# Moving the last result of a Strassen projection into tiles that an operand sum has left, with its residual loaded through another queue

## The chip, the cores and the metric

The kernel runs on one core of a Trainium2 chip, in one launch. The metric is the device time of that core in microseconds (us); runs of the same kernel are compared by their median. The profile is one such execution, recorded instruction by instruction.

## The reference

For each of 16 images, `x` is (512 channels, 1024 pixels) in f32. Group normalisation over 8 groups, a 1x1 convolution to queries, keys and values, attention with 4 heads of 128 channels over the 1024 pixels, a 1x1 output projection, and the residual:

```python
xn = ((xg - mu) * rsqrt(var + EPS)) * gamma + beta
q, k, v = split(einsum('oc,bchw->bohw', qkv_w, xn) + qkv_b, 3)
attn = softmax(einsum('bhnd,bhmd->bhnm', q, k) * scale)
out = einsum('bhnm,bhmd->bhnd', attn, v)
out = einsum('oc,bchw->bohw', proj_w, out) + proj_b
return x + out
```

## The kernel before

**The loop.** The work is written as 512 steps: 16 images, 4 heads, 8 blocks of keys. Each step has two halves, and each half issues one score matmul (`s`, L789, 128x512), its exponential on ScalarE (ACT, `p`, L795), and for the step before one weighted-sum matmul (`po`, L885). Every f32 matmul appears as two passes in the profile. Between these, `plan_head` hands out "units" of other work: queries and keys (`qk_`), values (`v_`), the projection of the image before (`pp_`), and the statistics and normalisation of the image after. A scheduler then orders the instructions of each engine by priorities (`tc.high_priority`) and by its own estimates, so the order on an engine is not the order of the source.

**Two Strassen levels.** `two_levels` multiplies a 512x512 weight by 512x1024 data with two levels of a Strassen scheme: seven outer products, done in four groups `OUTER = ((1, 5), (2, 6), (7, 4), (3,))`, numbered 0 to 3, and in each group seven inner products. `strassen` runs these in the order p1, p2, p6, p5, p7, p4, p3. Two PSUM banks, x and y, take the products; ACT copies x aside (`kept_copy`, L458, the tiles `pp_u` and `pp_p`), and VectorE (DVE) adds the parts into SBUF tiles `R` (`out_`, L584, `pp_r`). The inner operand sums t1 to t4 are DVE subtractions in `make_sum` (L534, `pp_t`, `qk_t`). Weight groups come by DMA on the queue of SyncE (SP), L371: two tiles a group, `w0` and `w1`, each in a pool of two buffers, so a load waits for the weights of two groups before.

**The outer sums of o.** The projection's data are the four heads' outputs (`os_`), and the outer sums t2, t3, t4 of them lie in single-buffered tiles of `tpool`: `ot20, ot21, ot30, ot31, ot40, ot41` (`halves`). The outer t4, which is `ot40` and `ot41`, is the operand of the outer product 4 alone, so only group 2 reads it: `ot40` holds the inner blocks b11 and b12, `ot41` holds b21 and b22. No other part of the kernel uses the tags `ot40` and `ot41`, and they are written again in the next image.

**The projection's results.** `proj_groups` gives eight 128x512 results an image: c11 (two), c22 and c21 (four), c12 (two). For each, `prepare` loads the residual block of `x` from DRAM into a tile (L756), `finish` adds R and the bias into it (L769), adds the second R (L772), and stores it (L773). `ready` calls `prepare` in the unit of p5 of group 1 (c11), group 2 (c22, c21) and group 3 (c12). All eight tiles come from `ypool`, tag `y`, four buffers used in turn, which the values' tiles `vt` and `vu` share. The load of a tile therefore waits until the store of the tile four places earlier has landed: c21 waits for c11, and c12 waits for c22. The loads and stores are issued on the queue of GpSimd (POOL), in order with POOL's small power instruction `rstd` (L67) of the next image's normalisation and with the loads of x and the copies of qk_t and v to DRAM.

**What stands around it.** `prepare` runs in the second head's part of an image (`plan_head`, h = 1) for images 0 to 14; the projection of image 15 is another function, `last_projection`. In the same stretch DVE takes part in the normalisation (L50 to L78), the running sums of p (`tot`, L803), and the first inner sums of the next image's queries and keys, `qk_t` (L534), without which TensorE (PE) can't start the products p5 of that group, `qk_y<-qk_t` (L564). ACT normalises the next image there (L85).

Of the kernel before, what the change touches and what calls it, by code (L numbers as in the profile page):

```python
# [10 lines left out]
F32 = mybir.dt.float32  # L11
# [5 lines left out]
P = 128  # L17
# [4 lines left out]
HALF = 512  # L22
# [140 lines left out]
def fast_path(ctx, tc, x, sources, out, consts, flag, dims):  # L163
# [6 lines left out]
    nc = tc.nc  # L170
# [10 lines left out]
    tpool = ctx.enter_context(tc.tile_pool(name="t", bufs=1))  # L181
# [7 lines left out]
    ypool = ctx.enter_context(tc.tile_pool(name="y", bufs=4))  # L189
# [556 lines left out]
    def proj_groups(b):  # L746

        ys = {}

        def place(which, r):  # L750
            return 2 * (int(which[1]) - 1) + r, int(which[2]) - 1

        def prepare(which, r):
            o, half = place(which, r)
            t = ys[which, r] = ypool.tile([P, HALF], F32, tag="y", name=f"y_{b}_{o}_{half}")
            dma = nc.gpsimd.dma_start(t, x[b, ts(o, P), ts(half, HALF)])  # L756

            tc.add_manual_dep(
                dma.ins, last_eviction[b].ins.name,
                mybir.DependencyInfo(  # L760
                    mybir.DependencyClass.Sync, mybir.DependencyReason.DATA
                ),
                reason="residual",
            )

        def finish(which, r, a, c):
            o, half = place(which, r)
            t = ys.pop((which, r))
            nc.vector.scalar_tensor_tensor(  # L769
                t, a, projb_sb[:, o : o + 1], t, ALU.add, ALU.add  # L770
            )
            nc.vector.tensor_add(t, t, c)  # L772
            nc.gpsimd.dma_start(out[b, ts(o, P), ts(half, HALF)], t)  # L773

        return two_levels(f"pp_{b}", "proj", b, lambda: ob[b], finish, prepare=prepare)
# [6 lines left out]
    def where(s):  # L782
        bh, j = divmod(s, NB)
        return (*divmod(bh, HEADS), j)
# [327 lines left out]
    for s in range(steps + 1):  # L1112
        units = []
        if s < steps:
            b, h, j = where(s)
# [159 lines left out]
```

## Time and profile before

| | |
|---|---|
| median of 7 runs | 3189.69 us (3188.1 to 3192.7) |
| the profiled execution's own time | 3190.44 us |
| its span, first to last instruction | 3188.7 us |
| PE busy | 3157.4 us, 99% of the span |
| DVE busy | 2632.9 us, 83% |
| ACT busy | 1443.7 us, 45% |
| POOL busy | 527.6 us, 17% |
| granted TensorE clock | 1.000 |
| `y<-in_x` loads on POOL (L756) | 120, of 256 KB, 3.9 us from issue to landing (median) |
| `w_proj<-kept_proj` loads on SP (L371) | 120 |

Time lies outside the span too: 3190.44 - 3188.7 = 1.7 us. In the lines of the profile, a row has the start in us, the length in us, the engine, the source line, the operation, and `out<-in` by the names of the tiles with their numbers left out; `x2` means that two equal instructions are merged. In brackets stands how long the engine was idle before it and what ended the idle time. One image takes some 196.3 us.

### The profile page before, as it was taken

The page shows a single profiled execution, that of the slowest core. Times are in us where ns is not written, and L with a number is a line of the kernel's source. Part 1 is how long each engine was busy: PE and PEld are TensorE (multiplying, and loading weights), DVE is VectorE, ACT ScalarE, POOL GpSimd, SP SyncE. Part 2 cuts the span into 40 slices and gives each one's busy share as a digit, 9 for nine tenths or more (in the row PEclk, how much of TensorE's full clock was granted, in tenths as well). Part 3 has the DMA queues.
Part 4 walks back from the last instruction along what each step waited for, and adds up shares of the span by engine and source line. Part 5 has one row for each costly group of instructions (what it writes and reads, how often), then busy time and mean ns, then how long its engine had stood idle before and what let it go on. Part 6 is the DMA issues. An engine that isn't in the chain of part 4 may idle for free.

```text
span 3188.7 us, 34047 instructions
## 1 busy us (share of the span) xinstructions
PE 3157.4 (99%) x10474; PEld 2183.5 (68%) x10474; DVE 2632.9 (83%) x4625; ACT 1443.7 (45%) x2709; POOL 527.6 (17%) x922
## 2 busy tenths in 40 slices
PE   8999999999999999999999999999999999999999
PEld 6566676776766766667666676667666676766764
DVE  8878978788887888878888787987879878788784
ACT  2535435354353543534435454453534545344342
POOL 0011221111211112211122111222112221122200
PEclk9999999999999999999999999999999999999999
DMA  5655554546545455454554546555455554555531
GB/s 168 208 185 160 185 177 144 179 143 199 166 156 168 155 186 175 157 166 145 193 171 162 172 135 196 166 173 173 134 182 169 175 180 131 183 158 186 180 126 41
DMA packets 209387, 526.92 MB, mean 165 GB/s; under 512 B 32816, under 2 KB 65840, under 8 KB 209200
## 3 DMA queue, kind: packets, MB, share of 16 engines
q1 hardware_dynamic: 128992, 276.88, 28.3%
q0 software_dynamic: 66240, 212.39, 19.8%
q10 hardware_dynamic: 13968, 35.41, 3.5%
q8 instruction: 86, 1.41, 0.2%
q14 instruction: 101, 0.83, 0.1%
HBM read 389.56 MB, written 135.00 MB: 165 GB/s over the span
## 4 chain that ended last, share of the span: by engine, by line
PE 87%; DVE 5%; issue 3%; DMA 2%; ACT 2%; POOL 1%; SPq 0%; POOLq 0%; DVEq 0%
PE po L885 24%; PE s L789 24%; PE qk_x L564 12%; PE qk_y L564 9%; PE v_x L564 6%; PE v_y L564 4%; PE pp_x L564 4%; PE pp_y L564 3%; ACT x L85 1%; DVE pp_r L631 1%; DMA y<-in_x 1%; POOL rstd L67 1%; DVE pp_r L584 1%; DVE tot L803 1%; DMA out_y<-y 1%
## 5 line engine op out<-in xcount | busy, mean ns | idle before, releaser
L885 PE MATMUL po<-p,v 128*128 128x512 f32 x2048 | 1048.9, 594 | 0.0
L789 PE MATMUL s<-qk,qk 128*128 128x512 f32 x2048 | 1047.1, 593 | 1.3 <-ACT p L795 1.3
L795 ACT ACTIVATE p<-s 128x512 f32<-128x512 f32 x1024 | 610.8, 597 | 945.5 <-PE s L789 903.8
L885 PEld LDWEIGHTS po<-p,v 128*128 128x128 f32 x2048 | 602.9, 303 | 316.8 <-issue 212.1
L803 DVE TENSOR_TENSOR tot<-tot,p 128x1024 f32<-128x1024 f32 x385 | 469.2, 1219 | 161.6 <-ACT p L795 161.6
L789 PEld LDWEIGHTS s<-qk,qk 128*128 128x128 f32 x2048 | 387.6, 190 | 89.2 <-issue 28.0
L564 PEld LDWEIGHTS qk_x<-qk_t,w 128*128 128x128 f32 x1344 | 250.6, 190 | 171.3 <-issue 76.6
L564 PE MATMUL qk_x<-qk_t,w 128*128 128x256 f32 x1344 | 357.3, 382 | 1.1 <-ACT qk_u L458 1.1
L458 ACT COPY qk_u<-qk_x 128x512 f32<-128x512 f32 (+1 forms) x256 | 136.3, 533 | 231.9 <-PE qk_x L564 227.4
L728 POOL DMA_DIRECT2D vd<-vu x120 | 66.6, 556 | 906.8 <-DVE vu L720 903.1
L584 DVE TENSOR_TENSOR qk_r<-qk_y,qk_u 128x512 f32<-128x512 f32 (+1 forms) x256 | 158.4, 619 | 36.1 <-ACT qk_u L458 21.8
L564 PE MATMUL pp_x<-pp_t,w_proj 128*128 128x256 f32 x630 | 169.3, 385 | 6.0 <-ACT pp_u L458 5.8
L773 POOL DMA_DIRECT2D out_y<-y x120 | 66.2, 551 | 615.8 <-DVE y L772 585.8
L733 POOL DMA_DIRECT2D v<-vd x240 | 140.5, 592 | 163.8 <-DMA vd<-vu 61.3
L584 DVE TENSOR_TENSOR v_r<-v_y,v_u 128x512 f32<-128x512 f32 (+1 forms) x120 | 75.7, 631 | 110.6 <-ACT v_u L458 80.3
L564 PE MATMUL v_x<-v_t,w_v 128*128 128x256 f32 x630 | 166.6, 381 | 0.0
L538 POOL DMA_DIRECT2D kept_t<-qk_t x240 | 129.2, 540 | 224.4 <-DVE qk_t L534 158.4
L564 PEld LDWEIGHTS pp_x<-pp_t,w_proj 128*128 128x128 f32 x630 | 115.4, 190 | 73.2 <-issue 22.2
L564 PEld LDWEIGHTS v_x<-v_t,w_v 128*128 128x128 f32 x630 | 118.4, 190 | 55.3 <-issue 19.1
L564 PE MATMUL qk_y<-x,w 128*128 128x256 f32 x512 | 141.8, 379 | 0.0
L663 DVE SCALAR_TENSOR_TENSOR qk<-qk_r,qkb_sb,qk_r 128x512 f32<-128x512 f32 x192 | 137.7, 745 | 1.6
L458 ACT COPY v_u<-v_x 128x512 f32<-128x512 f32 (+1 forms) x124 | 66.3, 535 | 160.4 <-PE v_x L564 130.3
(204 smaller groups left out, 4485.0 us busy)
## 6 DMA issues: line engine op xcount, KB each, us to landing
kept_t<-qk_t POOLq DMA_DIRECT2D x180, 256.0 KB, 3.0
w<-kept SPq DMA_DIRECT2D x90, 512.0 KB, 4.0
v_t<-kept_t SPq DMA_DIRECT2D x180, 256.0 KB, 2.8
w<-kept SPq DMA_DIRECT2D x90, 384.0 KB, 3.6
rinv<-row ACTq DMA_DIRECT2D x63, 512.0 KB, 4.8
x<-in_x POOLq DMA_DIRECT2D x60, 512.0 KB, 4.8
vd<-vu POOLq DMA_DIRECT2D x120, 256.0 KB, 3.1
v<-vd POOLq DMA_DIRECT2D x240, 128.0 KB, 4.1
```

What stands on the lines that cost most here:

```text
L458: nc.scalar.copy(t[n][:, :width], t["x"][:, :width])
L538: nc.gpsimd.dma_start(t, to)
L564: nc.tensor.matmul(acc[:, ts(i, Q)], have["w"][t][:, i, slot, :], inner(i, bn), start=(first and i == 0), stop=True, skip_group_check=True,)
L584: nc.vector.tensor_add(dst, view(a), view(c))
L663: nc.vector.scalar_tensor_tensor(st[b, h][:, ts(half, HALF)], a, qkb_sb[:, i : i + 1], c, ALU.add, ALU.add)
L728: nc.gpsimd.dma_start(rows[which][ts(h, P), :], u)
L733: nc.gpsimd.dma_start(vs[b, pair][ts(q, BLK), half].rearrange("m h (k i) j -> m (h k) (i j)", k=n), rows[which].rearrange("(k m) (q e) -> ...
L773: nc.gpsimd.dma_start(out[b, ts(o, P), ts(half, HALF)], t)
L789: nc.tensor.matmul(sc, ks[b, h][:, ts(j, P)], qs[b, h][:, ts(half, HALF)], start=True, stop=True)
L795: exps[s] = nc.scalar.activation(ps[s][:, ts(half, HALF)], sc, AF.Exp, scale=SCALE)
L803: added[b, h, j] = nc.vector.tensor_add(tot[b, h][:, i], tot[b, h][:, i], ps[s][:, i])
L885: nc.tensor.matmul(po[b, h][:, i], v_block(b, h, j), ps[s][:, i], start=(j == 0), stop=(j == NB - 1),)
```

## The change

The two c12 results of images 0 to 14 no longer take tiles of `ypool`. They take tiles of `tpool` under the tags `ot40` and `ot41`, and their residuals are loaded by a DMA on SP's queue. The loads of the other six results, the additions and all stores are as they were (stores on POOL's queue). `ypool` now gives 22 tiles an image in place of 24. Lines behind the edit move down by six: the load is L762, the additions are L775 and L778, the store is L779.

```diff
         def prepare(which, r):
             o, half = place(which, r)
-            t = ys[which, r] = ypool.tile([P, HALF], F32, tag="y", name=f"y_{b}_{o}_{half}")
-            dma = nc.gpsimd.dma_start(t, x[b, ts(o, P), ts(half, HALF)])
+
+            own = which == "c12"
+            t = ys[which, r] = (tpool if own else ypool).tile(
+                [P, HALF], F32, tag=f"ot4{r}" if own else "y", name=f"y_{b}_{o}_{half}"
+            )
+
+            eng = nc.sync if own else nc.gpsimd
+            dma = eng.dma_start(t, x[b, ts(o, P), ts(half, HALF)])
 
             tc.add_manual_dep(
                 dma.ins, last_eviction[b].ins.name,
```

## The prediction

> **What bounds the kernel now.** The first view is the page's busy times, the second its chain of work that ended last.
>
> ```profile
> PE 3157.4 (99%) x10474; PEld 2183.5 (68%) x10474; DVE 2632.9 (83%) x4625; ACT 1443.7 (45%) x2709; POOL 527.6 (17%) x922
> PE 87%; DVE 5%; issue 3%; DMA 2%; ACT 2%; POOL 1%; SPq 0%; POOLq 0%; DVEq 0%
> ```
>
> PE sets the time, so a change pays only where PE stands still. The third view is the waits, for PE alone:
>
> ```profile
> PE pp_x L564 <- ACT pp_u L458: 5.8, 14, 0.4
> PE qk_y L564 <- DVE qk_t L534: 3.6, 3, 1.8
> ```
>
> Outside the start these two are nearly all: 14 waits of 0.41 us, one in each image but the last, and three for DVE's qk_t. To see where DVE was late I read the groups of instructions for the tile y:
>
> ```profile
> L769 DVE SCALAR_TENSOR_TENSOR y<-pp_r,projb_sb,y 128x512 f32<-128x512 f32 x120 | 87.9, 748 | 6.3 <-DMA y<-in_x 5.5
> ```
>
> DVE waited 5.5 us for residual loads in all. The timeline says which ones. Image 5, by engine:
>
> ```profile
> 1321.74 1.15 POOL L773 DMA_DIRECT2D out_y<-y  x2 [5.69 <-DVE y L772]
> 1325.06 0.54 POOL L756 DMA_DIRECT2D y<-in_x  x1 [0.58 <-DMA out_y<-y]
> 1326.42 0.54 POOL L756 DMA_DIRECT2D y<-in_x  x1 [0.82 <-DMA out_y<-y]
> 1331.65 0.75 DVE L769 SCALAR_TENSOR_TENSOR y<-pp_r,projb_sb,y 128x512 f32<-128x512 f32 x1 [1.95 <-DMA y<-in_x]
> 1334.00 0.70 PE L564 MATMUL qk_y<-qk_t,w 128*128 128x256 f32 x2 [1.81 <-DVE qk_t L534]
> ```
>
> and image 6:
>
> ```profile
> 1523.25 1.20 POOL L756 DMA_DIRECT2D y<-in_x  x2 [0.47 <-DMA out_y<-y]
> 1527.27 1.47 DVE L769 SCALAR_TENSOR_TENSOR y<-pp_r,projb_sb,y 128x512 f32<-128x512 f32 x2
> 1529.86 0.42 DVE L534 TENSOR_TENSOR qk_t<-x 128x256 f32<-128x256 f32 x1
> 1529.90 1.13 PE L564 MATMUL qk_y<-qk_t,w 128*128 128x256 f32 x4
> ```
>
> Both loads are c12's: they wait until c22's stores have landed, and reach POOL only 4.0 us before DVE wants them (1523.25 to 1527.27). The same loads take 3.9 us to land at the median. So it is a race: in image 6 it is just won, in image 5 lost by 1.95 us, and 1.81 of it reaches PE. Image 6 shows one thing more. Four passes of this kind take 1.03 us elsewhere and 1.13 here: the second pair of `qk_y` waits some 0.1 us for `qk_t`, which ends at 1529.86 + 0.42 = 1530.28. DVE is just in time even where no load is late. The length of an image, from one `rstd` to the next, is in the chain in order of time:
>
> ```profile
> 1314.16 1.88 POOL rstd L67
> 1512.48 1.89 POOL rstd L67
> 1708.83 1.89 POOL rstd L67
> ```
>
> Image 5 takes 198.32 us, image 6 196.35. The later `rstd` give 196.30, 196.45, 196.31, 197.97, 196.81, 196.27. I take 196.30 as an image with no late load.
>
> **The late loads.** DVE's waits at L769 are 0.24, 0.29, 0.28, 1.95, 1.42, 0.45 us in images 1, 3, 4, 5, 10, 11, and 0.90 in image 14. Images 3, 4, 5, 10 and 11 lie 0.44, 0.36, 2.02, 1.67 and 0.51 us above 196.30. Images 1 and 2 are together 0.83 above, of which I give the wait in image 1 some 0.3; the rest is none of this. The wait in image 14 has no `qk_t` behind it and PE shows no wait: zero, at most 0.9. Sum 0.3 + 0.44 + 0.36 + 2.02 + 1.67 + 0.51 = **5.3 us**.
>
> **Whether they go.** In the built program's order on SP, the first c12 load stands between the two weight loads of projection group 3, the second between those of the next image's query group 0. Before, these lie at 1494.93 and 1504.42, and at 1507.86 and 1514.34 in image 6. The first load must wait for the last readers of `ot40`: group 2's p1 (PE, 1497.32 to 1498.35) and its t3 sums (DVE, to 1498.28), so it goes at about 1498.4, while the load behind it can't go before 1504.42 anyway. The second waits for group 2's p3, which is what `w1` behind it waits for too (1514.34): that load goes one issue, 0.32 us, later. Its weights are first read at the `qk_x` of 1533.46, 19 us on, so this costs nothing; if that cover were gone it would cost 0.32 an image, 4.5 in all.
>
> What the loads must beat: DVE's addition for the first is moved forward in the built order, into the slot of an outer sum of o (L280) at 1510.97, 12.6 us after the issue; the second's stands behind the first's second addition, about 1528.2, 13.9 us after. SP's loads of 256 KB have medians of 2.8 (`v_t<-kept_t`) and 3.2 us (`w_proj`), all loads of L371 2.2 to 9.1, the residuals on POOL 2.7 to 10.4. The highest is inside 12.6, so I take a wait of zero and a gain of 5.3.
>
> The Trainium skill, "DMA: Bandwidth & Descriptors", section "Issuing engines are not separate DMA queues", speaks against such a change: DMAs from any engine run on the same 16 DMA engines, and spreading them saves only issue time. By that rule alone this change is worth nothing, and the execution would stay at 3190.4. The rows say that the wait is for a tile to come free, not for a queue; by them it is 5.3.
>
> **Issue work.** POOL loses 30 issues of 0.54 us, SP gains 30 of 0.32. Neither is on the chain, and c21's last store, `kept_t` and `vd` on POOL stand behind two instructions fewer, which wait for DVE (903.1 us at L728). Zero.
>
> **DVE's new order.** The addition takes the place of the sum of o, that sum the place of a t3 sum of group 3, t3 that of t4, t4 that of the first `qk_t`; the first `qk_t` goes behind the second c12 addition. Counted from one row's start to the next, an addition takes 0.66, a sum of o 0.61, an inner sum 0.34. By the second `qk_t` the same instructions have run, so it ends at 1530.28 as before. In between, `sh` (L78, 1515.86) comes 0.05 + 0.27 = about 0.3 later. Behind it ACT is busy without a break to 1524.5, so the copy `pp_p` ends at about 1518.15 in place of 1517.83, and PE's p6, at 1518.02, may wait 0.3.
>
> **PE's new order.** In group 3, p4 and p3 go behind one `po` and one `s` more. The 0.41 wait (0.67 with what follows it: from `s` at 1521.47 to `po` at 1523.43 is 1.96, where 0.86 + 0.43 is the rule) goes, since `po` fills it until `pp_u` is there. So PE saves 0.67 and loses 0.3, and comes to the second `qk_y` pair about 0.4 early, and there it waits for 1530.28. What is late next is `qk_t`, and the gain is given back. Bounds an image: a loss of 0.3 if p6's wait is not swallowed, a gain of 0.67; times 14, +4.2 and -9.4. I take zero, since the row of 1529.90 shows the wait for `qk_t` already.
>
> **Sum.** 3190.44 - 5.3 = 3185.1. The profiled execution is 0.75 above the median of 3189.69, but a median run loses its own late loads too and should fall to the same floor, so the prediction is **3185.1 us**, 0.14% below the median. What this measurement can tell from no change is 0.2%, 6.4 us: faster begins below 3183.3, slower above 3196.1.
>
> **Rivals.** (1) *The floor holds*, as above: 3182 to 3187.5. Below 3185.1 lie 0.7 of excess that I gave to nothing (0.53 in images 1 and 2, 0.05 + 0.15 in two others), 0.9 of image 14 and 0.1 an image if the wait in the row of 1529.90 shrinks, 3.0 in all; above it lies about half of p6's price. (2) *PE keeps what p4 saves*: DVE is not what ends the stretch, because with no late loads it runs ahead by itself. For it: DVE has a 0.93 us gap before L69 where it could gain. Against it: that gap ends with POOL's `rstd`, which stands behind DVE's own chain, and the 1.13 row. 0.41 to 0.67 in 14 images is 5.7 to 9.4: 3175.7 to 3179.4. (3) *The load is hidden but another takes its place*: c21's loads (POOL, 1505.24 and 1509.70) still wait for stores, and the next operand after c12 is late by as much, or p6 waits the full 4.2: 3189 to 3190.4. For it: PE is 99% busy and DVE has no slack. Against it: c21's are first used at 1520.27 and 1521.87, 12 us or more after their issue. (4) *Slower*: the first load lands after DVE's early slot. DVE then stands at 1510.97 with the chain `pp_r`, `ve`, `rstd`, `sh` behind it, and ACT's normalisation behind that; each us is one of PE, 14 times. It decides from a landing of 12.6 us; slower by 0.2% needs 11 us over the floor, 0.8 an image, a landing of 13.4. At 14 us it would be 3185.1 + 14 x 1.4 = 3205. Against it: nothing in the rows above 10.4. That the edit does nothing is excluded: the load stands on SP in the built order.
>
> **Chances.** (1) 0.60, of which 0.15 lies below 3183.3; (2) 0.20; (3) 0.11; (4) 0.09. Faster is 0.15 + 0.20 = 0.35, same 0.45 + 0.11 = 0.56, slower 0.09. The range from 3178.5 to 3188.5 holds (1) whole, about a half of (2) and little of (3), and leaves out (4).
>
> **What would show it.** Right: no wait of L775 for `y<-in_x`; c12's loads issued on SP about 14 us before the `rstd` of the image (1498.4 against 1512.48) and 2 us after it; PE's three waits for `qk_t` of 1.8, 1.4 and 0.3 gone, but many of 0.2 to 0.5 at the same place, and none of `pp_x` for `pp_u`; images of 196.3 throughout. Wrong: images of 195.8 with no wait at `qk_y` (2), waits for other tiles (3), or DVE idle ahead of `ve` for `y<-in_x` (4).

## The result, and the profile after

The changed kernel takes 3181.79 us (median of 13 runs, 3180.58 to 3183.52), the kernel before 3191.18 us in the same comparison (median of 33, 3186.52 to 3197.61). The ratio is 0.9971, 95% interval 0.9964 to 0.9979: faster by 0.29%. The prediction was 3185.1 us in a range of 3178.5 to 3188.5; "same" was held likelier than "faster", and by the bound of 0.2% set there it is faster. The profiled execution took 3181.52 us with a span of 3179.7 us (before: 3190.44 and 3188.7).

Busy times and the chain of work that ended last, from the page of the kernel after:

```profile
PE 3157.4 (99%) x10474; PEld 2182.9 (69%) x10474; DVE 2630.0 (83%) x4625; ACT 1441.8 (45%) x2709; POOL 512.4 (16%) x892
PE 87%; DVE 10%; issue 1%; POOL 1%; DMA 1%; ACT 0%; SPq 0%; POOLq 0%; DVEq 0%
```

PE does the same 3157.4 us of work in a span that is 9.0 us shorter: only standing time went. PE's waits for `qk_t` (engine, tile and line, released by what; us in all, times, longest; the view lists waits of 0.15 us and more):

```profile
PE qk_y L564 <- DVE qk_t L534: 2.2, 14, 0.2
```

The line of 14 waits for `pp_u` is gone. In place of three long waits for `qk_t` there are fourteen of 0.15 us. The group of DVE's additions into y has no releaser left and 0.6 us idle, where it showed 6.3 us idle, 5.5 of it for `y<-in_x`:

```profile
L775 DVE SCALAR_TENSOR_TENSOR y<-pp_r,projb_sb,y 128x512 f32<-128x512 f32 x120 | 88.5, 748 | 0.6
```

`rstd` in the chain in order of time, from image 5 on:

```profile
1310.61 1.89 POOL rstd L67
1506.88 1.89 POOL rstd L67
1703.10 1.89 POOL rstd L67
```

196.27 and 196.22 us, where 198.32 and 196.35 stood. The timeline of image 6, SP and then DVE and PE (start, length, engine, line, operation, tiles, count):

```profile
1492.75 0.33 SPq L762 DMA_DIRECT2D y<-in_x  x1
1498.75 0.32 SPq L371 DMA_DIRECT2D w_proj<-kept_proj  x1
1502.20 0.32 SPq L371 DMA_DIRECT2D w<-kept  x1
1508.68 0.33 SPq L762 DMA_DIRECT2D y<-in_x  x1
1505.31 0.75 DVE L775 SCALAR_TENSOR_TENSOR y<-pp_r,projb_sb,y 128x512 f32<-128x512 f32 x1
1522.48 0.75 DVE L775 SCALAR_TENSOR_TENSOR y<-pp_r,projb_sb,y 128x512 f32<-128x512 f32 x1
1524.08 0.42 DVE L534 TENSOR_TENSOR qk_t<-x 128x256 f32<-128x256 f32 x1
1512.49 0.70 PE L564 MATMUL pp_x<-pp_t,w_proj 128*128 128x256 f32 x2
1524.55 0.70 PE L564 MATMUL qk_y<-qk_t,w 128*128 128x256 f32 x2 [0.15 <-DVE qk_t L534]
```

The two c12 loads go 14.1 us before `rstd` (1506.88) and 1.8 us after it, and are wanted 12.6 us (1505.31) and 13.8 us (1522.48) after their issue. Before, the issue was 4.0 us ahead of the use. The second `qk_y` pair starts at 1524.55, just after `qk_t` ends at 1524.50. The row of 1512.49 is p6, the product that now waits a little for `pp_p`.

**Where the 9.0 us of span came from.** The span is cut at the `rstd` of image 0 and at the last one, 13 images later. Up to the first cut the two profiles differ by 1.6 us (331.03 before, 329.42 after), in the 13 images by 6.7 (2557.92 and 2551.25), behind the last cut by 0.7 (299.73 and 299.00). Part of that is chance, as the further profiles show.

### The profile page after: what moved, and what is told of

Same layout as the page of the kernel before. It is cut to its first block, busy times and chain, and to the rows that moved or that the text cites. A ratio compares the mean times of both kernels' runs of the same rounds, so it can differ in the third digit from the quotient of the medians.

```text
span 3179.7 us, 34036 instructions
## 1 busy us (share of the span) xinstructions
PE 3157.4 (99%) x10474; PEld 2182.9 (69%) x10474; DVE 2630.0 (83%) x4625; ACT 1441.8 (45%) x2709; POOL 512.4 (16%) x892
## 4 chain that ended last, share of the span: by engine, by line
PE 87%; DVE 10%; issue 1%; POOL 1%; DMA 1%; ACT 0%; SPq 0%; POOLq 0%; DVEq 0%
PE po L891 24%; PE s L795 24%; PE qk_x L564 12%; PE qk_y L564 9%; PE v_x L564 6%; PE v_y L564 4%; PE pp_x L564 4%; PE pp_y L564 3%; DVE y L778 2%; DVE tot L809 2%; DVE y L775 2%; DVE pp_r L584 1%; DVE pp_r L631 1%; POOL rstd L67 1%; DVE o L901 1%
## 5 line engine op out<-in xcount | busy, mean ns | idle before, releaser
L779 POOL DMA_DIRECT2D out_y<-y x120 | 66.0, 550 | 632.0 <-DVE y L778 629.8
```

## The experiments

All are medians against the kernel before in the same group of runs; it had medians of 3190.3 to 3191.2 in the four groups. The kernel after was run in the first group alone, so a difference of one or two us between it and a variant is better read from the images than from the medians. "Image" is the mean of the 13 images in the profile; "loads" is DVE's wait at c12's first additions.

| kernel | median, us | ratio (95%) | image, us | loads, us |
|---|---|---|---|---|
| before, three profiles | 3190.3 to 3191.2 | | 196.76, 196.91, 196.69 | 5.5, 7.0, 4.2 |
| after | 3181.79 | 0.9971 (0.9964 to 0.9979) | 196.25 | 0 |
| tiles alone | 3182.0 | 0.9976 (0.9966 to 0.9985) | 196.24 | 0 |
| queue alone | 3187.77 | 0.9991 (0.9982 to 1.0000) | 196.75 | 4.5 |
| both, but the old wait | 3188.23 | 0.9994 (0.9985 to 1.0003) | 196.60 | 4.9 |
| both, order of before | 3182.32 | 0.9975 (0.9966 to 0.9985) | 196.31 | 0 |
| no c12 load at all | 3183.62 | 0.9979 (0.9970 to 0.9988) | 196.29 | - |
| load still later | 3211.14 | 1.0064 (1.0049 to 1.0080) | 198.10 | 51.3 |
| one more addition on DVE | 3184.40 | 0.9983 (0.9974 to 0.9992) | 196.47 | 0 |
| first sums urgent | 3184.27 | 0.9983 (0.9974 to 0.9993) | 196.43 | 0 |
| first sums 4 places earlier | 3183.50 | 0.9978 (0.9969 to 0.9987) | 196.39 | 0 |
| first sums 12 places earlier | 3183.97 | 0.9982 (0.9973 to 0.9991) | 196.40 | 0 |

### Tiles alone, queue alone

The change has two halves. The first kernel keeps the tiles `ot40` and `ot41` and loads through POOL's queue as before:

```diff
-            eng = nc.sync if own else nc.gpsimd
+            eng = nc.gpsimd
```

> c12 in the tiles ot40 and ot41, its residuals loaded on POOL's queue as before the change; PE, DVE and ACT have the changed kernel's order. (A) The gain comes from loads that no longer wait for c22's stores: they go 12 us ahead of their use, so 3.3 to 5.2 us of landing on POOL do no harm, and the time is the changed kernel's, 3181.8 within 1 us. (B) The gain comes from SP's queue, on which these loads land in 2.5 to 2.9 us: without it the kernel goes back towards 3191. (C) The gain comes from the order of DVE and PE, which is here as changed: 3181.8 too. The second load stands behind rstd on POOL, 13 us before its use, and costs nothing by any of them.

The second keeps SP's queue and takes the tiles from `ypool` again:

```diff
-            t = ys[which, r] = (tpool if own else ypool).tile(
-                [P, HALF], F32, tag=f"ot4{r}" if own else "y", name=...
+            t = ys[which, r] = ypool.tile([P, HALF], F32, tag="y", name=...
```

> c12 in ypool's tiles as before, its residuals loaded on SP's queue; the order on DVE, PE and ACT is that of the kernel before. The loads still wait for c22's stores and can go only 4.0 us ahead of their use. (A) The wait for the tile is there, so the late loads are too: 3188 to 3191. (B) On SP they land in 2.5 to 2.9 us, inside the 4.0: no DVE wait for y<-in_x, and 3182 to 3183. (C) The order is the old one, with the 0.41 us wait of PE for pp_u in each image: 3191, or 3187 where only the late loads go. By my forecast, which gave the queue nothing: 3190.

Tiles alone give 3182.0 us, within 0.2 us of the whole change. Queue alone gives 3187.77 us, some 2.9 below before, with an interval that ends at 1.0000. DVE's waits in the kernel with the queue alone:

```profile
DVE y L775 <- DMA y<-in_x: 4.5, 4, 2.5
```

So the loads stay late when only their queue changes. The tile that comes free early is the cause. The Trainium skill, "DMA: Bandwidth & Descriptors", section "Issuing engines are not separate DMA queues", by which alone the prediction had the whole change at nothing, agrees with this half: less than 0.2% for the queue.

One of the four late loads cost more than its wait. In image 2 PE stood for 2.33 us, and behind that the granted clock was 0.50 from 743 to 745 us and 0.76 from 745 to 747; the image is 4.24 us over 196.30, some 1.9 beyond the wait. In the next kernel PE stood for 2.67 us in the same image, the clock stayed at 1.00, and the image is 2.92 us over.

### Both, but the old wait

The kernel after, with each c12 load made to wait for the c22 store that it waited for before:

```diff
+            if own:
+                tc.add_manual_dep(
+                    dma.ins, stores["c22", r].ins.name, ...
```

> The changed kernel, but each c12 load is made to wait until the store of the c22 result of the same half has landed, as it had to before; the order on DVE, PE and ACT falls back to that of the kernel before. (A) The wait is back, and so is the time: 3188 to 3191. (B) SP's landing of 2.5 to 2.9 us is inside the 4.0 us: 3182 to 3183, as with the queue alone. (C) 3187 to 3191.

3188.23 us, and 4.9 us of waiting for the loads. With the new tiles and the new queue but the old moment of issue most of the gain is lost: some 2.5 of 8.7 us stays, as with the queue alone, and the interval holds 1. Four loads are late, in images 2, 6, 10 and 14 as with the queue alone. It is the moment that counts.

### Both, in the order of before

The new order on DVE could be a gain of its own. This kernel is the one after, with c12's first additions queued behind the last sum that stood ahead of them, which puts DVE's instructions into the order of before:

```diff
+            with ExitStack() as late_:
+                if which == "c12":
+                    late_.enter_context(tc.issue_after(added[b + 1, 1, NB - 1].ins))
...
```

> The changed kernel's tiles, queue and early loads, but c12's first additions are held behind the last running sum of p, so that DVE, PE and ACT have the order of the kernel before. (A) and (B): no late load, so 3181.8 plus at most 0.05 us in each of 14 images: 3181.5 to 3183. PE waits 0.41 us for pp_u in each image again and 0.1 for qk_t, in place of 0.15 for qk_t. (C) 3187 to 3191.

3182.32 us; images of 196.30, against 196.25. PE's waits:

```profile
PE pp_x L564 <- ACT pp_u L458: 5.8, 14, 0.4
```

The 14 waits for `pp_u` are back, the 14 for `qk_t` are gone, and the image is 0.05 us longer. What p4 saves in the new order is lost again at p6 and at `qk_y`, but for 0.05 us. It also confirms 196.30 as the length of an image with no late load in the old order.

### No load, and a later load

The kernel before without c12's residual load, and the kernel after with loads that wait for the last c21 store:

```diff
+            if which == "c12":
+                return
...
-                t, a, projb_sb[:, o : o + 1], t, ALU.add, ALU.add
+                t, a, projb_sb[:, o : o + 1], c if which == "c12" else t, ALU.add, ALU.add
```

> The kernel before, but the c12 results load no residual: the tile still comes from the four of ypool and still waits until c22's store of it has landed, and the first addition takes the second R in place of the residual (c12's residual is left out of the output; as many DVE instructions of the same shapes, in the order of before). It leaves the wait for the stores and takes the load's own 3 to 5 us away. Theory A (only the landing of the load against DVE's addition matters, a store that has landed 4 us earlier costs nothing): no wait of DVE for y, none of PE for qk_t beyond 0.2, the 14 waits of 0.4 for pp_u stay; the middle 13 images 2552.0 as in the kernel after with its old order, median about 3182.3. Rival (the stores on POOL's queue, or the tiles of ypool, hold something else up as well): images stay above 196.3 and the median at 3184 to 3190.

Images of 196.29 with the wait for c22's stores still there: a store that has landed in time costs nothing, and the excess over 196.30 goes with the loads (a small part of it was not c12's, as the further profiles of before show). The median of 3183.62 is 1.3 us over the one expected, with intervals that overlap.

```diff
+            if own:
+                tc.add_manual_dep(
+                    dma.ins, stores["c21", 1].ins.name, ...
```

> The kernel after, but the two c12 loads wait until the last c21 store of the image has landed (in the frame of image 6 about 1528, where DVE wants the first at 1527.3 in the order of before). Landing takes another 3.3 to 4.5 us, so the first addition is 4 to 5 us late in each of 14 or 15 images. Theory A (PE follows DVE one for one there, as in the images 5 and 10 of the kernel before, where 1.95 and 1.42 us of waiting cost 2.02 and 1.67): 14 x 4.1 to 14 x 5, so 57 to 70 us above 3181.8, 3239 to 3252. Rival (the order is planned anew around the late load and DVE has other work to put first, or PE's queue holds other units): a part of it is hidden, 3190 to 3225.

3211.14 us: the rival's 3190 to 3225 held, not the 3239 to 3252 of one for one. DVE waited 51.3 us for the loads, and the median rose by 29.3. From its waits, and from DVE's timeline in image 6:

```profile
PE qk_y L564 <- DVE qk_r L584: 11.9, 15, 0.9
1536.41 0.42 DVE L534 TENSOR_TENSOR qk_t<-x 128x256 f32<-128x256 f32 x1
1538.09 1.28 DVE L280 TENSOR_TENSOR xt<-x,x 128x512 f32<-128x512 f32 x2
1542.49 0.75 DVE L783 SCALAR_TENSOR_TENSOR y<-pp_r,projb_sb,y 128x512 f32<-128x512 f32 x1 [3.12 <-DMA y<-in_x]
```

The scheduler knew of this wait, and put most of the inner sums and two sums of x (L280) ahead of the late addition. PE then waits for the next thing behind it, `qk_r`, by 0.8 us an image, and 13 times for `qk_t` at `qk_x`, 2.9 us in all. So a late load cost about its full length where it came by chance into an order that does not allow for it (1.95 us of waiting and 2.02 of image in image 5 of the kernel before), and somewhat over half where the order was made for it.

### What is left at qk_t

After the change PE waits 14 times for `qk_t`. One more DVE addition of 128x512 ahead of it, in each image (c21's first half gets its second R twice):

```diff
+            if which == "c21" and r == 0:
+                nc.vector.tensor_add(t, t, c)
```

> The kernel after with one more DVE addition of 128x512 (some 0.6 us) at the first c21 result of each image, ahead of the first qk_t of the next image (c21's first half gets its second R twice). If DVE ends the stretch, as the prediction says (qk_y waits 0.2 for qk_t in 14 images), PE waits 0.6 more in each: 14 x 0.6 = 8.4, about 3190. If DVE has slack there that the 0.2 hides, or the new order puts other work behind: 3182 to 3185.

3184.40 us, 2.6 more and not 8.4; the image is 0.2 us longer where DVE has 0.6 us more to do. The second `qk_t` ends 0.6 us later against the `rstd`, as expected, but PE's order changed with it. From PE's timeline:

```profile
1525.40 0.67 PE L564 MATMUL qk_y<-qk_t,w 128*128 128x256 f32 x2 [0.15 <-DVE qk_t L534]
1525.90 1.02 PE L797 MATMUL s<-qk,qk 128*128 128x512 f32 x2
1526.76 0.59 PE L564 MATMUL qk_y<-qk_t,w 128*128 128x256 f32 x2
```

A score matmul of 0.86 us now stands between the two pairs of `qk_y`, and the wait is at the first pair. How late DVE is there depends on the planned order, not on its amount of work alone.

Then the other way round, the sums earlier. In three steps: urgent (shown), 4 places, 12 places:

```diff
-            for i in range(n):
...
+            with ExitStack() as early:
+                if sums == "keep" and g == 0 and m == "t1":
+                    early.enter_context(tc.high_priority(URGENT))
+                for i in range(n):
+                    nc.vector.tensor_sub(to[:, i, :], inner_block(g, i, a), inner_block(g, i, c))
```

> The kernel after, with the first inner sums of each image's queries (group 0, t1) planned ahead of the other DVE work as urgent, so that qk_t does not stand behind c12's additions. If the 14 waits of 0.2 at qk_y are all that DVE costs PE in the stretch, they go and nothing else comes: 14 x 0.2 = 2.8 less, 3179. If the order after the sums makes other work late by as much (sh, and ACT's normalisation behind it; or ot for the next group): 3181 to 3186. The order on PE is planned anew as well, so a new wait elsewhere may decide: then above 3186.

> The kernel after with the first inner sums t1 of an image's queries planned 4 places earlier: DVE's order stays as it is, on PE one score matmul goes ahead of the qk_y pair, and the second qk_y behind the next qk_x, so that the wait of 0.2 us for qk_t is filled. If PE's place before qk_t is all that is left, 14 x 0.15 to 0.2, so 2 to 3 us: images of 196.05 to 196.15, 3179 to 3180. If the next operand is as late (the qk_x that now comes earlier), the images stay at 196.25 and the median at 3181.8.

> The kernel after with the same sums planned 12 places earlier: on DVE both stand ahead of the last three c12 additions, and PE takes the four products p5 and p7 in turn ahead of the score matmul. If DVE's end at qk_t was the last wait of the stretch, it goes: 14 x 0.2 = 2.8 us, 3179. If PE needs the operand of p7, which is now early as well, before DVE has it, a wait of 0.2 to 0.4 comes back at qk_x, as it did with the urgent sums: 3182 to 3184.

(With 4 and 12 places the number stands for URGENT, and with 4 only the second of the two sums was given the priority.) PE's waits for the stretch, in the kernels urgent, 4 places and 12 places:

```profile
PE qk_x L567 <- DVE qk_t L537: 6.2, 14, 0.4
```

```profile
PE qk_x L567 <- ACT p L804: 3.7, 14, 0.3
```

```profile
PE qk_x L567 <- DVE qk_t L537: 5.7, 14, 0.4
```

In all three the wait at `qk_y` went, and fourteen waits at the next product came, each longer than the 0.15 us that went: images of 196.43, 196.31 (without one image of 197.36, in which `qk_y` waited 0.8 us for `qk_r`) and 196.40 against 196.25. (With 4 places the view names `p`, which ended 0.03 us after the `qk_t` of that product; which of the two held PE there is not settled.) The medians are 1.7 to 2.5 us above the kernel after, with intervals that overlap. None of these three orders beats it, so the fourteen small waits were not to be had by moving `qk_t` in these ways.

### The kernel before, twice more

> The kernel before, unchanged, for a second profile. If the term of 5.3 us was low because the profiled execution of before was a mild one, the excess of its images over 196.30 differs here, 7 to 10 us over the images 1 to 13, and with other images late by other amounts. If late loads cost 5 to 6 us again, the rest of the 8 to 9 us between the medians lies in the start or the end.

> The kernel before, unchanged, for a third profile: the same two readings as for the second. The late images should be others again if the moment of landing is chance, the same if the order decides it.

3190.66 and 3187.74 us. DVE's wait for the loads, and PE's for `qk_t`, in the second profile (which took about the median time):

```profile
DVE y L769 <- DMA y<-in_x: 7.0, 9, 2.1
PE qk_y L564 <- DVE qk_t L534: 5.1, 5, 2.0
```

In the third DVE waited 4.2 us for them in 5 waits, and PE 3.0 us for `qk_t` in 4.

The 13 images lie 6.0, 7.9 and 5.1 us over 13 x 196.30 in the three profiles. Images 4, 5 and 10 are late by 0.36 us or more in all three; image 3 is 0.44 over in the first alone. So the order makes some images likely to lose the race, and chance says by how much.

Not all of this excess is late c12 loads. Image 7 is 1.00 us over in the second profile and 0.44 in the third, but most of the first figure and all of the second comes later in the image: DVE waits until a copy of v to DRAM (`vd<-vu`) has landed, and PE then for `qk_r`, 0.47 and 0.18 us. DVE's row in the second profile:

```profile
1820.09 1.17 DVE L720 STREAM_TRANSPOSE vu<-vt 128x512 f32<-128x512 f32 x1 [1.45 <-DMA vd<-vu]
```

And at the start of image 2, in all three profiles, `rstd` stands on POOL behind c21's second load, which waits there for a store of c11. POOL in the first profile:

```profile
724.75 0.54 POOL L756 DMA_DIRECT2D y<-in_x  x1 [4.36 <-DMA out_y<-y]
725.30 1.03 POOL L67 TENSOR_TENSOR rstd<-ve,neghalf 128x4 f32<-128x4 f32 x1
```

`rstd` starts 1.4 to 1.5 us after DVE has finished its operand `ve`, where 0.15 is the rule; the normalisation and the copy `pp_p` come later by it, and PE's p6 waits for `pp_p`. Images 1 and 2 together are 0.39 and 0.48 us over in the second and third profiles, where PE shows no wait for `qk_t` in them. In every other kernel here `rstd` starts 0.15 us after `ve` in that place. So late c12 loads come to some 5.5 (6.0 - 0.5), 6.7 (7.9 - 0.4 - 0.8) and 4.2 us (5.1 - 0.5 - 0.4).

Up to the first cut the second and third need 329.74 us, the kernel after 329.42, the first profile 331.03: its start was 1.3 us longer than theirs, with the same code. Behind the last cut they need 299.25 and 299.23.

With the second profile the sum closes at the median: 3188.8 - 3179.7 = 9.1 us of span, of which 0.3 is the start, 7.9 the excess of the images (6.7 of it late loads), 0.65 (13 x 0.05) the new order and 0.25 the end.

## Why the prediction was right or wrong

**That the late loads are the term, and that they go: right.** The wait of L769 for `y<-in_x` is gone in all 30 results. The landing that had to beat 12.6 us was 2.5 to 4.4:

```profile
DMA to landing us min/median/max: 2.5/2.6/4.4
```

The first load goes 12.6 us before its use, as worked out, the second 13.8. That the wait was for a tile and not for a queue, which was read from POOL's rows, is shown by the two halves: 3182.0 and 3187.77.

**Their size, 5.3 us: right for the execution that it was read from, but not a constant.** Late loads cost some 5.5 us in that execution, 6.7 and 4.2 in the two others. Of the 0.7 that was left aside, some 0.5 is the wait of `rstd` in image 2. It was rightly not counted as a late load, but it goes as well: in every variant `rstd` starts on time there, also in the one with only c12's load left out. No run shows by itself what makes it go. Between the medians of before (3190.7) and of the kernel with the old order and no late load (3182.32) lie 8.4 us, near the excess of 7.9 in the second profile, which took the median time.

**"A median run loses its own late loads too and should fall to the same floor": the idea was right, but the floor was 3.6 us too high, and this is the step that failed.** The floor was 3190.44 less 5.3, and so kept what that execution had of its own. Against the profiled execution after, 3181.52, the difference is 1.6 us of the start (1.3 of them in no other profile of before), 0.7 behind the last cut, and in the images 0.7 of the excess left aside and 0.65 of the new order; that is 3.65. A floor counted up from quiet images would have been nearer than one counted down from a whole execution. Against the median of 3189.69 the forecast gain was 4.6 us, half of the 9.4 that were measured: 3.3 of the rest is the floor against the median after, and 1.5 is the median of before, which was 3191.18 in 33 runs where 3189.69 was that of 7.

**The new order: right, at nearly zero.** p4's wait went and came back at p6 and at `qk_y`, where `qk_t` ends at the same place in the order; 0.05 us an image stays, 0.7 us in all, inside the bounds of +4.2 and -9.4. p6's wait, priced at up to 0.3, is 0.13 (the score matmuls before it start at 1511.50, and the next start is due 0.86 later; p6 starts at 1512.49), and its pair then takes 0.70 us where 0.59 is the rule. The "many waits of 0.2 to 0.5" are fourteen of 0.15.

**Issue work and weight loads: right at zero.** The weights stand behind each other on SP as described, and PE shows no new wait for them.

**The rivals.** (1) came closest: its mechanism held, and 3181.79 lies just under the 3182 at which it was cut off. (2), that PE keeps p4's saving, falls: the wait for `qk_t` is in the trace, and three orders that take it away bring the next. (3) falls: no other load takes the place, PE's only new waits are the 0.15 at `qk_y` and the 0.13 at p6. (4), that the first load comes too late for its early slot, falls with a longest landing of 4.4 us; its price of one for one fits the waits that the order does not allow for (1.95 and 2.02 in image 5), and the later load shows 29.3 for 51.3 where it does.

**The chances.** "Faster" had 0.35. The bound of 3183.3 lay 1.8 us under the forecast, and the start and the end of the one profiled execution moved the floor by 1.6 and 0.7 us, together more than that and both to the same side; the forecast counted neither. The excess left aside stood in the bounds of (1), but not in the forecast.

## What to carry to other kernels

A load that waits for a buffer whose last store is still under way loses by chance, not by a constant: find the races (issue to use against issue to landing), take their loss from two or three executions if they are to be had, and count the floor up from the images in which all were won. Where the race is removed by giving the load a buffer that is free early, the queue hardly matters (here less than 0.2%). Not every excess of an image is such a race: look where in the image PE lost the time. Where PE waited for only 0.15 us at one operand, three ways of moving that operand forward each brought a longer wait at the next product.

## What the runs showed of the hardware

The landing of the same 256 KB load depends on the moment more than on its queue. On SP at the new moment the medians are 2.8 us (first load) and 2.5 (second); on SP at the old moment, with the queue alone changed, 4.0 and 4.0. On POOL at the new moment they are 3.1 and 3.5, at the old one 3.2 to 3.5 and 4.0 to 4.2. So SP was 0.3 to 1.0 us quicker at the new moment, and no quicker at the old. Two things differ between the moments. At the old one the two loads can be under way together (0.66 us apart in image 6 of the kernel before), at the new one each goes alone. And other transfers are on their way, which shows in the DMA engines' busy share (the last two columns are that share and GB/s), one to three us behind the issue of a c12 load. In the kernel before:

```profile
1525.00:1526.00 1.00, 1.00 (x3) 0.61 (x2) 1.00 (x3) 0.14 (x1) 0.52 (x1) 1.00 0.96 279
```

In the kernel after, for the first load and for the second:

```profile
1494.00:1495.00 1.00, 1.00 (x4) 0.74 (x4) 0.79 (x1) 0.73 (x2) 0.00 (x0) 1.00 0.65 205
1510.00:1511.00 1.00, 1.00 (x5) 0.72 (x4) 1.00 (x4) 0.47 (x2) 0.00 (x0) 1.00 1.02 341
```

These shares hold the load's own 256 KB, and the second load lands soonest (2.5 us) with the highest of them. So the share alone does not tell how long a load takes; no run here changed the traffic alone, and what makes the difference stays open.
